# Edges of the adder layers, full-width products beside the projection, and the load order and ending of a scan, in a four-layer kernel on one Trainium2 core

## The chip, the cores and the metric

The kernel runs as one program on one core of one Trainium2 chip. The metric is the device time of one execution in microseconds (us). The profile gives the span from the first to the last instruction, the instructions of each engine, and the granted clock of TensorE. PE is TensorE's matrix products and PEld its weight loads, DVE is VectorE, ACT is ScalarE, POOL is GpSimd, and SP is the engine that issues most DMAs; a letter q behind an engine's name means its DMA queue. On this chip a float32 product is recorded as two passes, so counts of matmuls in the profile are twice those of the source.

## The reference

The input is four images of 128 channels and 64 x 64 pixels, in float32. Four layers follow each other:

```python
# layer 0: attention over the 4096 pixels of an image
attn = softmax(einsum('bci,bcj->bij', q, k)); x = gamma * einsum('bcj,bij->bci', v, attn) + x
# layer 1: twice a 3x3 convolution with weights rounded to powers of two, and an adder convolution
wq  = sign(w) * 2 ** round(log2(abs(w))), zero where abs(w) < 0.005
p   = conv3x3(x, wq)
out = -sum over taps and channels of abs(patch(p) - w_add)          # for each of 128 outputs
out = batchnorm(out)          # statistics over all images and pixels; relu after the first
x   = relu(second out + residual)
# layer 2: layer norms, a depthwise convolution with pooled attention, a feed-forward network
# layer 3: a selective scan
m      = sigmoid(illum_w . [x, illumination] + illum_b);  f_low = x * m
f_high = x * (1 + alpha * gradient)
xs, z  = split(in_proj(rms_norm(f_high)))
xs     = silu(causal_conv1d(xs, 4 taps))
dt, Bm, Cm = x_proj(xs);  delta = softplus(dt_proj(dt) + b)
# a forward and a backward scan of 16 states for each of 256 channels
h = exp(delta * A) * h + delta * Bm * xs;   y = sum over states of h * Cm + D * xs
out = layer_norm(out_proj(y * silu(z))) + gamma * f_low
```

## The kernel before

The layers run one after the other; each holds its data in SBUF and hands over through DRAM tensors (x1d, y1d, y2d, low_d, xs_d, sz_d, delta_d, du_d, xdbl_d, y_d) or, between layers 2 and 3, in four SBUF images `xp`. Channels lie on the 128 partitions, pixels along the free axis, and BK = 512 pixels make one block, 8 blocks one image. Instructions that are wrapped in `then` (keep_in_program_order) keep the order of the source on their engine. Those that are not wrapped, most DMAs of SP among them, are placed by the framework's scheduler before the program is built.

**Layer 1** (`layer1`, `shift_adder`). Both filters are loaded and quantized in `quantized` (L287) and `quantize` (L266 to L278), nine DVE instructions of 128 x 1152 each. `shift_adder` is called twice, with tags a1 and a2. It loads `w_add` (L306), makes negated copies (L311), small selection matrices (L316 to L320) and, on PE, the sums `wsum` of the weights (L335). Then the convolution of the first image runs alone: per block nine products from `xin` into one of three PSUM banks `pc` (L375), copied to the padded image `pb` by DVE (L380). The loop over 4 x 128 outputs follows the hand-written list ORDER. Per output, ACT makes absolute differences (`absolute`, L456), DVE makes maxima (`maximum`, L470; `added`, L462; `pair`, L479), and PE sums each over the channels into the PSUM banks `pa` (`summed`, L425). `pair` makes two half tiles from a ring `am` of seven, and a DMA that POOL issues adds one to the other (L481). Beside this loop a generator `beside` brings in the sums over the image (L396) and the next image's convolution, three steps for every four outputs. `evacuate` adds `wsum`, takes the statistics (L437, L440) and stores the outputs (L442). At the end `batchnorm_scale` sends the statistics to the DRAM tensor stats_d (L543), reads them back in another layout (L546), and aggregates them (L550). The second call normalizes its input blocks as they land (L571 to L575).

**Layer 3's preparation** (`layer3_prepare`). `split(b)` works block by block: one full product with `iwm` (L1053) and a one-row product with the illumination row (L1054) for the sigmoid, a one-row product with the gradient row (L1056), the sigmoid on ACT (L1058), `fh` (L1059) and the low part `sg` (L1061) on DVE, and a store to low_d (L1062). `norm(b)` (L1070 to L1081) is the root-mean-square norm. `project(b)` makes four pieces: products `px` copied to `pre` by ACT (L1099, L1100), four convolution passes of DVE (L1122, L1124), products `pz` through Silu (L1106, L1108) stored to sz_d, and Silu of the piece (L1127). `steps_of(b)` makes `xd` with 40 columns (L1143, L1146), `dv` from its first 8 rows (L1155, L1158), and softplus with Abs, Exp and Ln (L1160, L1161, L1169), and stores delta_d and du_d. For each image `project(b)`, `split(b + 1)` and `steps_of(b)` follow one another; `norm(b + 1)` runs beside the steps. The tiles `dv`, `ee` and `uu` have three buffers each, PSUM eight banks.

**Layer 3's scan** (`layer3_scan`). There are 128 tiles, 32 an image, of 8 channels and 16 states each, with two halves of 2048 pixels. Per half, `delta` loads `dl` and `products_in` loads `du`, spread over the partitions; `inputs` multiplies `du` by B on POOL (L1343). ACT makes the decays `da` (L1350), DVE scans (L1364), PE adds both directions (L1379), ACT copies (L1388), POOL multiplies by C (L1392). Loads are issued on SP in the order of the source. `finish` makes the output blocks (L1455 to L1475) of the image before, and after the last tile those of the last image.

Of the kernel before, what the change touches and what calls it, by code (L numbers as in the profile page):

```python
# [9 lines left out]
F32 = mybir.dt.float32  # L10
# [7 lines left out]
P = 128  # L18
B = 4
# [242 lines left out]
def quantize(nc, sb, w, of, name):  # L262

    flat = [P, TAPS * P]
    aw = sb.tile(flat, F32, tag="qa", name=f"{name}_aw")
    nc.vector.tensor_scalar(aw.bitcast(I32), w.bitcast(I32), 0x7FFFFFFF, None, ALU.bitwise_and)  # L266

    pw = sb.tile(flat, F32, tag="qp", name=f"{name}_pw")
    nc.vector.tensor_scalar(pw.bitcast(I32), w.bitcast(I32), 0x7F800000, None, ALU.bitwise_and)
    up = sb.tile(flat, F32, tag="qu", name=f"{name}_up")  # L270
    nc.vector.scalar_tensor_tensor(up, pw, 1.4142135381698608, aw, ALU.mult, ALU.is_lt)
    nc.vector.scalar_tensor_tensor(pw, up, 1.0, pw, ALU.add, ALU.mult)
    nc.vector.scalar_tensor_tensor(pw, aw, 0.005, pw, ALU.is_ge, ALU.mult)
    sg = sb.tile(flat, I32, tag="qu", name=f"{name}_sg")
    nc.vector.tensor_scalar(sg, w.bitcast(I32), -0x80000000, None, ALU.bitwise_and)
    nc.vector.tensor_tensor(pw.bitcast(I32), pw.bitcast(I32), sg, ALU.bitwise_or)
    nc.vector.tensor_tensor(pw, pw, w, ALU.subtract)
    nc.vector.tensor_tensor(of, w, pw, ALU.add)  # L278


def quantized(tc, pool, w_shift, tag):

    nc = tc.nc
    wqs = pool.tile([P, TAPS, P], F32, name=f"{tag}wq")
    with tc.tile_pool(name=f"{tag}q", bufs=1) as qp:
        ws = qp.tile([P, TAPS * P], F32, name=f"{tag}ws")
        nc.sync.dma_start(ws, w_shift)  # L287
        quantize(nc, qp, ws, wqs.rearrange("p t o -> p (t o)"), tag)
    return wqs


def shift_adder(tc, cm, load, wqs, w_add, stats, y_d, tag):
# [10 lines left out]
    with ExitStack() as ctx:  # L303
        cp = ctx.enter_context(tc.tile_pool(name=f"{tag}c", bufs=1))
        wa = cp.tile([P, TAPS, P], F32, name=f"{tag}wa")
        nc.sync.dma_start(wa.rearrange("p t o -> p (t o)"), w_add)  # L306
        wn = {}
        for t, scale in [(t, 1.0) for t in ABS_TAPS[0]] + [(ABS_TAPS[c][i], 0.5) for c, i in HALF.items()]:
            if (t, scale) not in wn:
                wn[t, scale] = cp.tile([P, P], F32, name=f"{tag}wn{t}_{len(wn)}")  # L310
                nc.vector.tensor_scalar(wn[t, scale], wa[:, t, :], -scale, None, ALU.mult)  # L311

        pick = {}
        for v in (-1.0, -2.0):
            pick[v] = cp.tile([P, 63], F32, name=f"{tag}pick{int(-v)}")
            nc.vector.memset(pick[v], 0.0)  # L316
            nc.vector.memset(pick[v][:, 31:32], v)
        third = cp.tile([P, 32], F32, name=f"{tag}third")
        nc.vector.memset(third, 0.0)
        nc.vector.memset(third[:, 2:32:4], 1.0)  # L320
# [5 lines left out]
        with tc.tile_pool(name=f"{tag}w", bufs=1) as wt:  # L326
            w_third = wt.tile([P, P], F32, name=f"{tag}wthird")
            nc.vector.memset(w_third, 0.0)
            nc.vector.tensor_copy(w_third[:, 2:P:4], wa[:, MAX_TAPS[3], 2:P:4])
            pw = ps_c.tile([P, NC], F32, tag="cv", name=f"{tag}pw")  # L330
            for c in range(NC):
                for g in range(4):
                    for i, t in enumerate(sum_taps):
                        w = w_third if t == MAX_TAPS[3] else wa[:, t, :]
                        nc.tensor.matmul(  # L335
                            pw[32 * g : 32 * g + 32, c : c + 1], w[:, 32 * c : 32 * c + 32], cm.one_col,
                            start=(i == 0), stop=(i == len(sum_taps) - 1), skip_group_check=True,
                        )
            nc.vector.tensor_copy(wsum, pw)
# [64 lines left out]
        def beside(b, pb_of):  # L404

            yield from sums_of_p(b, pb_of[b], sp_of[b])
            if b < B - 1:
                pb_of[b + 1] = padded(b + 1)
                yield from convolution(b + 1, pb_of[b + 1])

        pb_of, sp_of = {0: padded(0)}, {}
        for _ in convolution(0, pb_of[0]):
            pass
# [19 lines left out]
        def evacuate(chunk):  # L433
            b, c = divmod(chunk, NC)
            for k in range(2):
# [6 lines left out]
                nc.sync.dma_start(to[k], o)  # L442

# [29 lines left out]
        def pair(n, h):  # L473
# [7 lines left out]
            then(nc.gpsimd.dma_start(ms[1], ms[0], accum_op=ALU.add))  # L481
# [53 lines left out]
def layer1(ctx, tc, cm, w_shift1, w_add1, g1, b1, w_shift2, w_add2, g2, b2, x1d, y1d, y2d, stats_d):  # L535
# [5 lines left out]
    def batchnorm_scale(stats, at, gamma, name):  # L541

        nc.sync.dma_start(at, stats.rearrange("p c s v -> p c (s v)"))  # L543
        byco = lp.tile([P, 4, 2 * B * 6], F32, name=f"byco{name}")
        for c in range(4):
            nc.sync.dma_start(  # L546
                byco[32 * c : 32 * c + 32], at[:, c, :].rearrange("(g j) s -> j g s", g=4)
            )
# [11 lines left out]
    wq1, wq2 = quantized(tc, lp, w_shift1, "a1"), quantized(tc, lp, w_shift2, "a2")  # L560
# [6 lines left out]
    shift_adder(tc, cm, plain, wq1, w_add1, stats1, y1d, "a1")  # L567
    mean1, sc1 = batchnorm_scale(stats1, stats_d[0], vec["g1"], "1")
# [11 lines left out]
    shift_adder(tc, cm, normed, wq2, w_add2, stats2, y2d, "a2")  # L580
    mean2, sc2 = batchnorm_scale(stats2, stats_d[1], vec["g2"], "2")
# [422 lines left out]
def layer3_prepare(  # L1004
    tc, cm, xp, maps_d, illum_w, illum_wl, illum_b, rms_w, in_w, conv_w, conv_b, x_w, dt_w, dt_b,
    alpha, gamma, low_d, xs_d, sz_d, delta_d, du_d, xdbl_d,
# [3 lines left out]
    with ExitStack() as ctx:  # L1010
# [14 lines left out]
        ga = load([P, 1], gamma.partition_broadcast(P), "ga")  # L1025
# [4 lines left out]
        xw = load([P, 2, NX], x_w, "xw")  # L1030
        dtw = load([DT_RANK, 2 * P], dt_w, "dtw")
# [7 lines left out]

        fh_of, xs_of = {}, {}  # L1040

        def split(b):

            fh = big.tile([P, N], F32, tag="fh", name=f"fh{b}")
            fh_of[b] = fh
# [669 lines left out]
```

## Time and profile before

| | us |
|---|---|
| median of 3 runs | 21133.91 |
| lowest and highest run | 21114.99 and 21178.35 |
| the profiled execution's own time | 21155.93 |
| its span | 21154.1 |

| stage of the profiled execution | from | to |
|---|---|---|
| layer 0 | 0 | 1980 |
| layer 1, start | 1980 | 2025 |
| first adder layer: convolution of image 0, then the loop | 2025, 2091 | 9404 |
| between the adder layers | 9404 | 9438 |
| second adder layer: convolution of image 0, then the loop | 9438, 9504 | 16840 |
| between layer 1 and layer 2 | 16840 | 16889 |
| layer 2 | 16889 | 17883 |
| layer 3, preparation | 17883 | 18520 |
| scan: start, then the loop | 18520, 18574 | 21080 |
| scan: ending | 21080 | 21154 |

Over the whole span PE is busy for 93%, DVE for 90%, ACT for 83% and POOL for 36% of the time, and the mean granted clock is 0.966. These shares are means over stages with different limits; what an edit is worth is read in its own stage. In a line of the order of instructions, the numbers are the start and the length in us, and the bracket at the end gives the engine's idle time just before and what ended it.

### The profile page before, as it was taken

To read this page: it belongs to the slowest core of one execution; us is meant where nothing else is said; L and a number is where in the kernel's file an instruction comes from. 1 tells how busy PE (TensorE), PEld (TensorE's weight loads), DVE (VectorE), ACT (ScalarE), POOL (GpSimd) and SP (SyncE) were. 2 spreads that over 40 slices of the span, in tenths; PEclk is the share of its full clock that TensorE was granted. 3 is DMA by queue.
4 is the path that set the end of the run, shared out by engine and by line. 5 is a ranking of instruction groups with operands and counts; after the bars stand their busy time and mean duration, and the time that the engine had idled before them with its cause. 6 is when DMAs were issued, how large, how long until landed. Compare 5 with 4: busy or idle time off the path is not lost.

```text
span 21154.1 us, 323001 instructions
## 1 busy us (share of the span) xinstructions
PE 19660.1 (93%) x139180; PEld 6292.0 (30%) x139180; DVE 18970.2 (90%) x12273; ACT 17550.0 (83%) x9055; POOL 7577.3 (36%) x3844
## 2 busy tenths in 40 slices
PE   9998999999999999999999999999999877789998
PEld 4443222222222222222222222222222223223333
DVE  7876999999999999989999999999999887799998
ACT  5664999999999999989999999999999833466666
POOL 5665222222222222212222222222222100189998
PEclk9999999999999999999999999999999988699999
DMA  0000777777777777767777777777777710389997
GB/s 13 9 9 20 147 152 148 147 154 149 151 145 152 150 143 151 156 136 145 150 148 152 149 148 151 147 149 147 147 154 153 162 21 20 130 238 251 253 253 218
DMA packets 576191, 2970.17 MB, mean 140 GB/s; under 512 B 164572, under 2 KB 165476, under 8 KB 240804
## 3 DMA queue, kind: packets, MB, share of 16 engines
q0 software_dynamic: 296800, 2160.20, 51.0%
q1 hardware_dynamic: 277812, 787.19, 13.0%
q8 instruction: 1089, 17.84, 0.3%
q14 instruction: 346, 2.83, 0.0%
q10 hardware_dynamic: 144, 2.10, 0.0%
HBM read 662.03 MB, written 128.78 MB: 37 GB/s over the span
## 4 chain that ended last, share of the span: by engine, by line
PE 43%; issue 15%; DMA 14%; DVE 14%; ACT 11%; POOL 3%; SPq 1%; DVEq 0%; POOLq 0%; ACTq 0%
PE a1pa L425 15%; PE a2pa L425 13%; DMA ma<-ma 10%; ACT aa L456 9%; PE pe L164 4%; PE pav L207 4%; DVE h L1364 4%; DVE ma L479 3%; DVE da L470 2%; DMA du<-du_d 2%; DVE g L854 1%; POOL ma L481 1%; PE mg L1379 1%; DMA dl<-delta_d 1%; PE a1pc L375 1%
## 5 line engine op out<-in xcount | busy, mean ns | idle before, releaser
L481 POOL DMA_DIRECT2D ma<-ma x2048 | 3799.7, 1870 | 10892.9 <-DVE ma L479 7671.8
L456 ACT ACTIVATE aa<-a1pb,a1wn 128x4096 f32<-128x4096 f32 x1920 | 6959.4, 3711 | 485.5 <-PE a1pa L425 342.0
L456 ACT ACTIVATE aa<-a2pb,a2wn 128x4096 f32<-128x4096 f32 x1920 | 6964.9, 3712 | 358.9 <-PE a2pa L425 340.4
L425 PE MATMUL a1pa<-aa,a1pick 128*32 128x512 f32 x30720 | 3616.8, 600 | 84.4 <-ACT aa L456 81.3
L425 PE MATMUL a2pa<-aa,a2pick 128*32 128x512 f32 x30720 | 3617.2, 600 | 82.6 <-ACT aa L456 81.3
L470 DVE TENSOR_SCALAR da<-a2pb,a2wa 128x4096 f32<-128x4096 f32 x1408 | 3271.0, 2350 | 316.1 <-PE a2pa L425 316.1
L470 DVE TENSOR_SCALAR da<-a1pb,a1wa 128x4096 f32<-128x4096 f32 x1408 | 3269.6, 2350 | 306.8 <-PE a1pa L425 306.5
L425 PE MATMUL a1pa<-da,a1pick 128*32 128x512 f32 x22528 | 2696.1, 597 | 15.2 <-DVE da L470 15.2
L425 PE MATMUL a2pa<-da,a2pick 128*32 128x512 f32 x22528 | 2680.8, 594 | 18.0 <-DVE da L470 18.0
L479 DVE TENSOR_SCALAR ma<-a1pb,a1wa 128x2048 f32<-128x2048 f32 x2048 | 2529.8, 1282 | 71.1 <-DMA ma<-ma 71.1
L479 DVE TENSOR_SCALAR ma<-a2pb,a2wa 128x2048 f32<-128x2048 f32 x2048 | 2530.6, 1282 | 63.5 <-DMA ma<-ma 63.3
L1379 PE MATMUL mg<-h,ident 128*128 128x512 f32 x4096 | 1955.8, 615 | 214.6 <-ACT m L1388 174.0
L1364 DVE TENSOR_TENSOR_SCAN h<-da,h,dbu 128x1024 f32<-128x1024 f32 x768 | 1804.3, 2349 | 126.1 <-ACT da L1350 32.2
L425 PEld LDWEIGHTS a1pa<-aa,a1pick 128*32 128x32 f32 x30720 | 982.4, 111 | 2492.5 <-issue 2130.5
L425 PEld LDWEIGHTS a2pa<-aa,a2pick 128*32 128x32 f32 x30720 | 983.1, 111 | 2488.0 <-issue 2132.9
L425 PE MATMUL a2pa<-ma,a2pick 128*32 128x512 f32 x8192 | 1094.2, 607 | 266.0 <-DMA ma<-ma 265.8
L425 PE MATMUL a1pa<-ma,a1pick 128*32 128x512 f32 x8192 | 1096.2, 608 | 239.1 <-DMA ma<-ma 239.1
L201 POOL TENSOR_TENSOR ssum<-ssum,et 128x512 f32<-128x512 f32 x960 | 1230.0, 1281 | 233.0 <-ACT et L196 166.1
L425 PEld LDWEIGHTS a1pa<-da,a1pick 128*32 128x32 f32 x22528 | 716.9, 110 | 1747.2 <-issue 1612.4
L425 PEld LDWEIGHTS a2pa<-da,a2pick 128*32 128x32 f32 x22528 | 714.8, 110 | 1739.7 <-issue 1584.1
L462 DVE SCALAR_TENSOR_TENSOR aa<-a2pb,a2wa,aa 128x4096 f32<-128x4096 f32 x256 | 1147.4, 4482 | 81.8 <-ACT aa L456 81.7
L462 DVE SCALAR_TENSOR_TENSOR aa<-a1pb,a1wa,aa 128x4096 f32<-128x4096 f32 x256 | 1147.4, 4482 | 78.2 <-ACT aa L456 78.0
(295 smaller groups left out, 17707.1 us busy)
## 6 DMA issues: line engine op xcount, KB each, us to landing
ma<-ma POOLq DMA_DIRECT2D x2048, 1024.0 KB, 8.9
dl<-delta_d SPq DMA_DIRECT2D x256, 512.0 KB
dl<-delta_d SPq DMA_DIRECT2D x512, 256.0 KB
du<-du_d SPq DMA_DIRECT2D x256, 512.0 KB
du<-du_d SPq DMA_DIRECT2D x512, 256.0 KB
sz_d<-sz SPq DMA_DIRECT2D x64, 256.0 KB
xs_d<-xs SPq DMA_DIRECT2D x8, 2048.0 KB
delta_d<-dv SPq DMA_DIRECT2D x32, 512.0 KB
```

The lines of the kernel that those rows point to most:

```text
L164: nc.tensor.matmul(pe, k[:, bass.ts(j, P)], unit[u, "q"], start=True, stop=True)
L201: nc.gpsimd.tensor_tensor(unit[u, "sum"], unit[u, "sum"], at, ALU.add)
L207: nc.tensor.matmul(unit[u, "av"], image[u // NB][2][:, j, :], at, start=(j == 0), stop=(j == NJ - 1))
L375: then(nc.tensor.matmul(pc, wqs[:, t, :], here[:, y : y + RB, x : x + W], start=(t == 0), stop=(t == TAPS - 1),))
L425: then(nc.tensor.matmul(pa[k][32 * g : 32 * g + 32, :], pick[v][:, 31 - jj : 63 - jj], d[:, bass.ts(4 * at + g, BK)], start=(n // 32, k) n ...
L456: then(nc.scalar.activation(rows(at), view(n, t), AF.Abs, bias=bias, scale=scale))
L462: then(nc.vector.scalar_tensor_tensor(rows(at), view(n, ADDED_TAP), weight(n, ADDED_TAP), rows(at), ALU.max, ALU.add))
L470: then(nc.vector.tensor_scalar(rows(dt), view(n, t), weight(n, t), None, ALU.max))
L479: then(nc.vector.tensor_scalar(rows(mt), v, weight(n, t), None, ALU.max))
L481: then(nc.gpsimd.dma_start(ms[1], ms[0], accum_op=ALU.add))
L1364: then(nc.vector.tensor_tensor_scan(t[:, cols][:, s], da[:, s], st[n, "dbu", h][:, cols][:, s], 0.0 if e % 4 == 0 else st["last"], ALU.mul ...
L1379: then(nc.tensor.matmul(pm, cm.ident, st[n, way, h][:, bass.ts(k, BK)], start=(way == 0), stop=(way == 1)))
```

## The change

In layer 1, `quantize` becomes a generator that works in the ring `am`. Only the first layer's filter is quantized before the first convolution; the second layer's goes in four lots into that convolution, and `w_add`, its negated copies and `w_third` are loaded and made there. The sums of the weights become a generator `sums_of_w` in `beside` of image 0. The last output's pair is not added by a DMA: both half tiles are summed by PE. The statistics go by DMA from `stats` straight into `byco` in SBUF, chunk by chunk, and the last chunk's on two queues. `stats_d` is gone.

In layer 3's preparation, one-row products and those with 8 rows or 40 columns are made full-width with zeros: `xw`, `dtw`, `iwr`, `alr` and four map rows are zero-filled tiles of 128 rows. `split` is divided: `high(b)` makes only `fh`, into the image `xp[b - 1]` that is no longer needed, and for the next image stands in `project`, two blocks a piece; `low(b)` makes all eight sigmoid products, then the sigmoids in ACT and the product on POOL, and for the next image stands at the end of `project`. The factor gamma moves to the end of the scan.

In the scan, the first loads come in another order, and the last image's output has an ending of its own.

```diff
-def quantize(nc, sb, w, of, name):
+def quantize(tc, pool, w_shift, of, name):
+    w, aw, pw, up = [
+        pool.tile([P, HL], F32, tag="am", name=f"{name}_q{k}")[:, 0 : TAPS * P] for k in range(4)
+    ]
+    nc.sync.dma_start(w, w_shift)
+    yield
+    then(nc.vector.tensor_scalar(aw.bitcast(I32), w.bitcast(I32), 0x7FFFFFFF, None, ALU.bitwise_and))
...
         def beside(b, pb_of):
 
             yield from sums_of_p(b, pb_of[b], sp_of[b])
+            if b == 0:
+                yield from sums_of_w(w_third)
...
-        for _ in convolution(0, pb_of[0]):
-            pass
+        quantizing = [quantize(tc, mp, w, of, f"{tag}{k}") for k, (w, of) in enumerate(shifts)]
+        for q in quantizing[:1]:
+            for _ in q:
+                pass
+        for at, _ in enumerate(convolution(0, pb_of[0])):
+            if at == 0:
+                nc.sync.dma_start(wa.rearrange("p t o -> p (t o)"), w_add)
+                for q in quantizing[1:]:
+                    next(q)
+            if at % TAPS == 4 and at > 2 * TAPS:
+                for q in quantizing[1:]:
+                    next(q, None)
+            if at == 2 * TAPS + 1:
+                negated()
...
+            if b == B - 1:
+
+                for g in range(4):
+                    (nc.scalar if c == NC - 1 and g % 2 else nc.sync).dma_start(
+                        byco[32 * c : 32 * c + 32, g, :],
+                        stats[32 * g : 32 * g + 32, c, :, :].rearrange("p s v -> p (s v)"),
+                    )
...
-            then(nc.gpsimd.dma_start(ms[1], ms[0], accum_op=ALU.add))
+            if n < B * P - 1:
+                then(nc.gpsimd.dma_start(ms[1], ms[0], accum_op=ALU.add))
+            else:
+
+                streams[n, "q", h] = (-2.0, ms[0], (h,))
             streams[n, "p", h] = (-2.0, ms[1], (h,))
...
-        nc.sync.dma_start(at, stats.rearrange("p c s v -> p c (s v)"))
-        byco = lp.tile([P, 4, 2 * B * 6], F32, name=f"byco{name}")
-        for c in range(4):
-            nc.sync.dma_start(
-                byco[32 * c : 32 * c + 32], at[:, c, :].rearrange("(g j) s -> j g s", g=4)
-            )
...
+        def padded(shape, name):
+            t = cp.tile(shape, F32, name=name)
+            nc.gpsimd.memset(t, 0.0)
+            return t
+
+        xw = padded([P, 2, P], "xw")
+        nc.sync.dma_start(xw[:, :, 0:NX], x_w)
+        dtw = padded([P, 2 * P], "dtw")
+        nc.sync.dma_start(dtw[0:DT_RANK, :], dt_w)
...
+        map_rows = [[padded([P, BK], f"map{i}_{j}") for j in range(2)] for i in range(2)]
+
+        def map_row(i, b, k):
+            t = map_rows[i][k % 2]
+            nc.sync.dma_start(t[0:1, :], maps_d[i, b, bass.ts(k, BK)].rearrange("(o n) -> o n", o=1))
+            return t
...
+        def low(b):
+
+            halves = []
+            for k in range(NB):
+                pm = ps.tile([P, BK], F32, tag="mm", name=f"pm3_{b}_{k}")
+                then(nc.tensor.matmul(pm, iwm, inner(xp, b, k), start=True, stop=False))
+                then(nc.tensor.matmul(pm, iwr, map_row(0, b, k), start=False, stop=True))
+                halves.append(pm)
+            yield
+            for k2, tag in enumerate(("dv", "ee", "uu", "dv")):
+                sg = sb.tile([P, 2 * BK], F32, tag=tag, bufs=3, name=f"sg{b}_{k2}")
+                for i in range(2):
+                    then(nc.scalar.activation(sg[:, bass.ts(i, BK)], halves[2 * k2 + i], AF.Sigmoid, bias=ib))
+                src = xp[b][:, 2 * RB * k2 : 2 * RB * (k2 + 1), :].rearrange("p h w -> p (h w)")
+                then(nc.gpsimd.tensor_tensor(sg, src, sg, ALU.mult))
+                nc.sync.dma_start(low_d[b, :, bass.ts(k2, 2 * BK)], sg)
+
+        def high(b):
+
+            if b == 0:
+                fh = big.tile([P, N], F32, tag="fh", name="fh0")
+            else:
+                fh = xp[b - 1].rearrange("p h w -> p (h w)")
             fh_of[b] = fh
             for k in range(NB):
...
+                pg = ps.tile([P, BK], F32, tag="mm", name=f"pg{b}_{k}")
+                then(nc.tensor.matmul(pg, alr, map_row(1, b, k), start=True, stop=True))
                 yield
-                then(nc.vector.scalar_tensor_tensor(rows(sg), src, ga, rows(sg), ALU.mult, ALU.mult))
-                nc.sync.dma_start(low_d[b, :, c], sg)
+                then(nc.vector.scalar_tensor_tensor(
+                    rows(fh[:, bass.ts(k, BK)]), rows(pg), 1.0, inner(xp, b, k), ALU.add, ALU.mult
+                ))
...
-        def project(b):
+        def project(b, beside, behind):
...
                 if i + 1 < len(pieces):
                     projected(*pieces[i + 1])
+                next(beside, None)
+                next(beside, None)
...
                 for k in range(NB // 2):
                     gated(mc, h * NB // 2 + k)
+                if i + 1 == len(pieces):
+                    next(beside, None)
+                    next(behind, None)
                 then(nc.scalar.activation(xc, xc, AF.Silu, bias=cb[:, mc : mc + 1]))
                 if h == 1:
                     nc.sync.dma_start(xs_d[b, mc], xs_of[b, mc])
+            next(behind, None)
...
-        for _ in split(0):
+        for _ in high(0):
             pass
         cm.ln_and_exp(tc)
         for _ in norm(0):
             pass
+        for _ in low(0):
+            pass
         for b in range(B):
-            project(b)
-            if b < B - 1:
-                for _ in split(b + 1):
-                    pass
+            more = b < B - 1
+            project(b, high(b + 1) if more else iter(()), low(b + 1) if more else iter(()))
...
         for h in range(2):
-            delta(0, h)
             products_in(0, h)
             by_states(0, 0, h)
-        for h in range(2):
+            delta(0, h)
             inputs(0, h)
+        products_in(1, 0)
+        delta(1, 0)
+        products_in(1, 1)
+        for h in range(1, -1, -1):
             by_states(0, 1, h)
-            products_in(1, h)
...
-        going, k, t = [], 0, 0
-        while going or k < NB:
...
+        for k in range(NB + 1):
+            v = f"_last{k}"
+            if k < NB:
+                ck = bass.ts(k, BK)
+
+                t = big.tile([P, 4, BK], F32, tag="h", bufs=6, name=f"end{v}")
+                moved(t[:, 2, :], low_d[B - 1, :, ck])
+                for c in range(2):
+                    moved(t[:, c, :], y_d[B - 1, c, :, ck])
...
+                sq = sb.tile([P, BK], F32, tag="rs4", bufs=4, name=f"sq{v}")
+                then(nc.scalar.activation(sq, po, AF.Square))
+                then(nc.vector.tensor_scalar(t[:, 2, :], t[:, 2, :], ga, lb, ALU.mult, ALU.add))
+                ends[k] = (t, po, sq)
+            if k > 0:
...
+                then(nc.scalar.activation(rs, pv, AF.Ln, bias=cm.eps))
+                then(nc.scalar.activation(rs, rs, AF.Exp, scale=-0.5))
+                then(nc.vector.scalar_tensor_tensor(t[:, 3, :], po, lw, rs, ALU.mult, ALU.mult))
+                then(nc.vector.tensor_tensor(t[:, 3, :], t[:, 3, :], t[:, 2, :], ALU.add))
+                nc.gpsimd.dma_start(out[B - 1, :, bass.ts(k - 1, BK)], t[:, 3, :])
```

## The prediction

> **What bounds the kernel now.** I read first the busy time by stage, then the order of instructions on each engine at every seam between stages, then the list of waits in layer 3's preparation. By stage (start:end and length in us; then busy us of PE, PEld, DVE, ACT, POOL; granted clock, DMA share, GB/s):
>
> ```profile
> 1980.00:2025.00 45.00, 7.82 (x192) 7.69 (x193) 22.26 (x34) 0.00 (x0) 0.80 (x6) 0.50 0.20 60
> 2091.00:9404.00 7313.00, 6981.32 (x62224) 2043.94 (x62228) 6855.90 (x3804) 6960.51 (x1921) 1874.26 (x1059) 0.98 0.74 150
> 9404.00:9438.00 34.00, 12.81 (x228) 8.45 (x220) 7.65 (x23) 2.25 (x4) 1.68 (x7) 0.59 0.47 104
> 9504.00:16840.00 7336.00, 6970.93 (x62232) 2040.05 (x62236) 6873.55 (x3829) 6979.87 (x1944) 1932.36 (x1059) 0.99 0.74 149
> 16840.00:16889.00 49.00, 4.40 (x32) 0.57 (x24) 13.78 (x18) 6.54 (x5) 1.35 (x3) 0.55 0.71 244
> 17990.00:18018.00 28.00, 28.00 (x31) 7.89 (x30) 8.68 (x13) 7.37 (x10) 0.00 (x0) 0.50 0.38 151
> 18520.00:18574.00 54.00, 9.98 (x16) 4.36 (x16) 21.68 (x30) 9.76 (x9) 18.00 (x4) 0.52 0.98 246
> 18574.00:21080.00 2506.00, 2313.47 (x6760) 799.02 (x6760) 2378.18 (x1078) 1731.16 (x2159) 2339.95 (x555) 0.99 0.89 246
> 21080.00:21154.00 74.00, 36.21 (x81) 11.04 (x80) 1.38 (x2) 25.51 (x41) 24.74 (x17) 0.76 0.36 121
> ```
> The two adder loops (7313 and 7336 us) and the scan (2506 us) hold 17155 of 21154 us; in the loops PE, ACT and DVE are each at 94 to 95%. The change leaves these loops' instructions alone but for a few products. It works on the seams, where the engines wait: 45, 34, 49, 54 and 74 us, and on layer 3's preparation (17883 to 18520). There the order on PE reads:
>
> ```profile
> 17897.76 2.08 PE L1053 MATMUL pm<-x,iwm 128*128 128x512 f32 x2
> 17899.77 2.07 PE L1054 MATMUL pm<-mr,iwr 1*128 1x512 f32 x2
> 17901.63 1.91 PE L1056 MATMUL pg<-mr,alr 1*128 1x512 f32 x2
> ...
> 17933.12 3.78 PE L1074 MATMUL pv<-sq,mean 128*128 128x512 f32 x4 [1.01 <-ACT sq L1070]
> ```
> A block of `split` takes 5.71 us of PE, without a gap; its six passes take 0.95 us each. In the projection 16 such passes take 7.03 us, 0.43 each. So `split` is PE-bound at half clock: PE is busy for 28.00 of 28 us and the clock is 0.50. Two thirds of its products have one row. At layer 1's seams the waits are on transfers:
>
> ```profile
> 9426.16 1.02 DVE L550 BATCH_NORM_AGGREGATE mv<-byco 128x2 f32<-128x192 f32 x1 [0.58 <-DMA byco<-stats_d]
> 9432.85 71.13 SPq L571 DMA_DIRECT2D a2xin<-y1d  x11
> 9438.45 65.03 PE L375 MATMUL a2pc<-a2xin,a2wq 128*128 128x512 f32 x144 [5.67 <-ACT a2xin L575]
> 16878.51 2.41 DVE L673 TENSOR_SCALAR x<-x,mv,sc 128x4096 f32<-128x4096 f32 x1 [6.44 <-DMA x<-y2d]
> ```
>
> **Layer 1's start: -30.** Now: x1d's last block at 1980.1, the first filter lands and is quantized by 1994.87, then the second (14.2 us), then w_add (3.7) and its sums (8.2 of PE), then the input block (4.0); the convolution starts at 2025.02. After: only the first quantizing stands ahead, the input lands beside it, and the convolution starts at 1994.9. The second filter's nine DVE passes (10.4 us) go into the convolution, where DVE works 5.79 of 66 us, in four lots of about 3 us. A `pc` copy queued behind a lot is at most 3 us late, three banks of 7.7 us each cover that, and PE goes on; without the cover it would be 4 x 3 us. w_add is asked for after three input blocks and is wanted 17 us later. Bounds -33 to -27.
>
> **The sums of w inside the loops: +10.** 96 products (192 passes, 8.2 us) for each of two layers now stand among the adder products, on a PE that is 95% busy. Nothing if they fall into its gaps, 17 if each pushes the end. The chain of waits goes over PE more than over any other engine, so I take above half. They run in the first 20 of 92 side steps, and 93 fit, so the next image's convolution is still in time.
>
> **First to second adder layer: -18.** The last pair is no longer added by a transfer (9406.08 to 9413.27) but by 8 passes more for each half (1.04 us each), so the last statistics are ready at about 9410.8, not 9416.77. Then they went to DRAM (issued 9416.84), came back (9423.03), and were aggregated at 9426.16; now four issues on two queues (0.44 us each) go to SBUF straight and land, like `iw` (2.1 us from issue), at 9413.5. With 1.02 + 0.29 + 1.28 + 0.35 us the scale is there at 9416.5. The input block can be asked for when y1d's last store has landed, 9413.7 (issued at 9411, 2.7 us as `delta_d`'s takes), lands in 3.9 and is normalized in 1.5: PE starts at 9419, not 9438.45. I take 18 of the 19; the bounds are 10 (the store takes the 6.2 us that stats_d took, and more) and 22. [...]
>
> **Second adder layer to layer 2: -14.** The flush is 6 us shorter in the same way. SP's load of image 0 (16869.77) stood behind the DRAM round trip (16863.85); now 13 loads of 0.5 us stand ahead of it, so it goes out near 16853.5, and lands 8.7 us later as now, or up to 4 more beside `res`. Bounds -18 to -5.
>
> **Layer 3's preparation: -77.** *Image 0, -6.* `high(0)` is 8 products of 1.9 us, each waiting for one row in one of two buffers (2.3 us from issue): 4.2 us for two, 17 for all, instead of 46. Eight POOL fills (about 4 us, by 0.23 for 132 columns) fit in the time of the loads. `norm(0)` stays. `low(0)` then adds 32 passes, 14 us at 0.43, that `split` had inside; and the first convolution waits for the first `pg`, queued behind 8 projections: 4.5 us. 29 - 14 - 4.5, with 4 lost to cold passes: -6. *Three transitions, -65.* Image 3 has no `split` behind it: from the last convolution pass (18445.74) to the first `Abs` (18449.28) it takes 3.5 us; image 1 takes 40.3 (18138.77 to 18179.07). So a `split` costs 36.8. After: 8 `fh` passes inside `project` (8 x 0.69 = 5.5, DVE being the bound there: 52.2 of 53 us), and ACT's table load and 8 sigmoids at its end (1.28 + 8 x 0.69 = 6.8); `low`'s 32 passes lie under ACT's and DVE's last piece. The product moves to POOL (4 x 2.34 us), idle there. That is -24.5; I take off 3 for new waits: `fh` waits for its map row, with the four passes of the piece behind it and ACT's Silu waiting for those; a row waiting on SP for its buffer holds back sz_d stores, for which ACT waits (46.3 us today); the third `dv` waits for `sg`'s store. *Full-width steps, -6:* `pxd` and `pd` at 0.95 a pass lose some 1 to 2 us for each of 3 parts and 4 images, where DVE waits for them. Bounds -30 (rows late in each piece) to -105 (6 + 3 x 24.5 + 25).
>
> [...]
>
> **The scan's start: -2.** The first product needs `du` and B; `dl` goes behind them, so the first scan starts some 6 us sooner. But the DMA share is 0.98 from 18520 to 18574, and the twelve loads before tile 1's second half are the same bytes. What is won is waited for there. Bounds -8 to +4.
>
> **The scan's end: -22.** Now two blocks at a time wait for loads (PE 2.7 to 5.7 us each time), and end at 21148.7 plus 5.4 for the last store. After, loads run six blocks ahead: 8 x 768 KB at 240 GB/s is 26 us from 21090, against PE's 3.0, ACT's 1.9 and DVE's 2.0 a block. Then 7 us for the last block, and 7 for a store from POOL (the least for `ma` is 6.9): 21131, not 21154. Bounds -28 to -10.
>
> Sum: -30 + 10 - 18 - 14 - 77 - 2 - 22 = -153; with every bound at its worst -61, at its best -214. The profiled execution took 21155.93 (span 21154.1), 22 above the median 21133.91 of the runs; I take the sum off the median: 20981.
>
> **The rivals.** *The clock stays at half in spite of the zeros* (for: the added rows do no work; against: `pxd`, 128 rows by 40, brings 0.45 a pass at 18025). `low(0)` then costs 15 more, each hidden `low` 10, the steps win nothing: -153 + 51 = -102, 21032. *Rows, stores and banks hold the preparation* (for: 46.3 us of Silu waiting for sz_d; against: SP issued rows between stores in `split`). Each later piece waits 8 us for its rows, 72 in all, and `low`'s rows come behind the last store, 13 us three times: -153 + 111 = -42, 21092. *The adder loop gets slower* by its order: the quantizer takes eight tiles of the `am` ring of seven, so layer 1's pairs sit one buffer on, and the sums delay PE, and three engines at 95% do not catch up. Its price is per channel: 1024 channels of 14.3 us; from 0.15 us each (1.0%) it eats the whole gain, from 0.21 the kernel is slower by over 0.3%. For it: the two layers' loops differ by 23 us with the same code; against it: that is 0.04 us a channel. At 0.25 it is 21237.
>
> **How the numbers follow.** A run of this kernel can tell 0.3%, 63 us, from no change. The forecast has 0.67, the clock 0.14, the held preparation 0.11, the slower loop 0.06; 0.02 stays for more than all of it. The forecast alone spans 20920 to 21073; reaching to the held preparation, and with 15 us of the runs' spread below, 20905 to 21090. Faster: the first two and the rest, 0.83; within 0.3%: most of the held preparation, 0.10; slower: the loop and a worse hold, 0.07.
>
> **What would show it.** Right: convolutions at 1995 and near 9394 (9419 less 30, and 5 for the sums), loops still 7313 to 7345 us, one-row products gone and the clock above 0.8 in the projection, no stretch between image 1's last convolution pass and its first `Abs` above 17 us, a tail of 50 us. Wrong: a loop longer by 60 us, `fh` waiting for `pg` by over 5 us a piece, or POOL fills or the last store on the chain.

## The result and the profile after

The changed kernel is slower, by little: 21181.64 us as the median of 20 runs (21154.04 to 21223.47), against 21143.69 for 20 runs of the kernel before, ratio 1.0019 with a 95% interval of 1.0012 to 1.0025. The forecast was 20981 us. The profiled execution took 21184.28 us (span 21182.5), 28.4 more than the profiled one of before in span.

The same view as before, busy time by stage (start:end and length in us; busy us of PE, PEld, DVE, ACT, POOL; granted clock, DMA share, GB/s), of the changed kernel:

```profile
1980.00:1996.00 16.00, 0.27 (x1) 0.30 (x2) 10.24 (x9) 0.00 (x0) 0.99 (x12) 0.50 0.69 186
2064.00:9461.00 7397.00, 6986.45 (x62452) 2050.77 (x62456) 6851.48 (x3803) 6955.81 (x1919) 1929.60 (x1058) 0.98 0.74 148
9461.00:9477.00 16.00, 2.02 (x21) 0.54 (x14) 5.20 (x8) 4.13 (x6) 1.06 (x12) 0.69 0.42 112
9545.00:16964.00 7419.00, 7000.82 (x62452) 2051.29 (x62456) 6869.87 (x3828) 6975.80 (x1944) 1979.10 (x1058) 0.98 0.73 148
...
18032.00:18048.00 16.00, 14.61 (x34) 6.07 (x34) 1.52 (x4) 8.33 (x12) 7.03 (x3) 1.00 0.20 82
...
21116.00:21182.50 66.50, 43.20 (x109) 14.83 (x107) 16.68 (x26) 18.72 (x30) 14.36 (x11) 0.76 0.40 135
```

The seams did shrink. But each adder loop now takes about 7400 us, 84 more than before, and DVE and ACT have no more work in it. Of the 168 us of both loops together, 138 are more idle time of PE and 30 more busy time: what grew is mostly waiting. By marks that both traces have (first adder product, the start of the last chunk's first evacuation, the first normalization of layer 2, its last `pf` product, the first and the last scan), the 28.4 us are made up so:

| stretch | before, us | after, us | measured | forecast |
|---|---|---|---|---|
| up to the first adder product | 2094.6 | 2063.9 | -30.6 | -30 |
| first loop | 7313.3 | 7397.3 | +83.9 | +10 for both |
| first to second adder layer, with the convolution | 100.1 | 84.1 | -16.0 | -18 |
| second loop | 7334.6 | 7418.8 | +84.2 | (above) |
| second adder layer to layer 2 | 35.9 | 28.8 | -7.1 | -14 |
| layer 2 | 1004.6 | 1008.3 | +3.7 | 0 |
| preparation, up to the first scan | 660.5 | 590.9 | -69.6 | -77 and -2 |
| scans | 2526.2 | 2523.4 | -2.8 | 0 |
| behind the last scan | 84.3 | 67.0 | -17.3 | -22 |

Without the loops the sum is -140, where -163 was forecast. The loops took back 168, and they did it in one place. Cut at the evacuations, image 0 of the two layers goes from 1884.8 and 1897.8 us to 1978.6 and 1989.3 (+94 and +92), and images 1 to 3 together from 5428.5 and 5436.9 to 5418.7 and 5429.5. The windows of one chunk in image 0 and one in image 1 show it; of before:

```profile
2612.00:3064.00 452.00, 441.10 (x3892) 131.00 (x3888) 428.47 (x239) 434.91 (x121) 110.98 (x66) 0.99 0.76 153
...
4448.00:4906.00 458.00, 441.64 (x3896) 131.13 (x3892) 429.24 (x240) 435.68 (x121) 121.93 (x66) 0.99 0.75 152
```
and of after:

```profile
2620.00:3100.60 480.60, 443.62 (x3892) 130.46 (x3888) 428.86 (x241) 435.12 (x121) 135.83 (x67) 0.97 0.72 144
...
4512.00:4962.50 450.50, 438.58 (x3892) 131.09 (x3888) 428.70 (x239) 435.16 (x121) 111.60 (x66) 1.00 0.77 154
```
The chunk of image 0 has 28.6 us more, though PE works only 2.5 us more and DVE and ACT no more; POOL, which makes nothing new there, has 25 us more. Only image 0 has `sums_of_w`.

In ORDER a token names an output of a group of four, a kind and an index: 1P1 is output 1's pair (P) for half 1 of the image, M a maximum, S the maximum added to an absolute difference, A an absolute difference, and C the place of the three side steps; a small letter is PE's sum of the same. "Held" is said here of an issue of the adding DMA that takes POOL over 8 us. How a stall of PE comes about is read from the order of instructions (start, length, what; in the bracket the idle time before and what ended it). DVE of after:

```profile
2682.89 0.69 DVE L377 COPY a1pb<-a1pc 128x512 f32<-128x512 f32 x1 [2.63 <-PE a1pc L372]
...
2699.59 4.61 DVE L491 TENSOR_SCALAR da<-a1pb,a1wa 128x4096 f32<-128x4096 f32 x2
2704.11 2.48 DVE L500 TENSOR_SCALAR ma<-a1pb,a1wa 128x2048 f32<-128x2048 f32 x2
2706.50 4.62 DVE L491 TENSOR_SCALAR da<-a1pb,a1wa 128x4096 f32<-128x4096 f32 x2
...
2720.34 2.35 DVE L491 TENSOR_SCALAR da<-a1pb,a1wa 128x4096 f32<-128x4096 f32 x1
```
POOL's issues of the adding DMA, and PE, at the same time:

```profile
2695.58 0.86 POOL L503 DMA_DIRECT2D ma<-ma  x1 [4.83 <-DVE ma L500]
2707.12 17.47 POOL L503 DMA_DIRECT2D ma<-ma  x3 [10.69 <-DVE ma L500]
```
```profile
2729.09 1.93 PE L439 MATMUL a1pa<-ma,a1pick 128*32 128x512 f32 x8 [10.27 <-DMA ma<-ma]
```
DVE copies a block of image 1's convolution right behind its last product and waits 2.63 us for it. From there on it runs without a pause. POOL's issue for pair 1P1 (the first of the three in the 17.47 us) begins at 2707.12 and ends at 2722.8, when DVE's run ends: 15.7 us, and PE stands for 10.27. The clock falls with it: it is granted at 0.5 from 2722.38 to 2732.61, so the eight passes at 2729.09 take 1.93 us where eight like them took 1.04 at 2707.48. At the same place of ORDER in the kernel before, an earlier group, DVE and then POOL:

```profile
2186.95 2.35 DVE L470 TENSOR_SCALAR da<-a1pb,a1wa 128x4096 f32<-128x4096 f32 x1
2189.52 2.35 DVE L470 TENSOR_SCALAR da<-a1pb,a1wa 128x4096 f32<-128x4096 f32 x1 [0.23 <-PE a1pa L425]
```
```profile
2180.41 11.58 POOL L481 DMA_DIRECT2D ma<-ma  x2 [10.45 <-DVE ma L479]
```
There DVE waits 0.23 us for PE, and the issue ends in that gap, after 9.0 us; PE stands for 2.7. In image 0 the changed kernel has 11 and 9 stalls of PE of 9 to 12 us, the kernel before none. Added up over both loops, PE stood for 287 us before products of 1P1 whose issue had been held, and for 102 in the kernel before; in image 0 of the two layers it is 209 against 19, and image 0 is 185 us longer.

Why the copy stands there: `beside` is advanced by three steps at each token C. Before, 12 steps of `sums_of_p` came ahead of image 1's convolution, so every copy fell on the first step of a token, a whole group of four outputs behind its product. The eight steps of `sums_of_w` make that 20, and every copy of image 1 falls on the third step, behind products given out in the same token.

### The profile page after: what moved, and what is told of

Its sections match the earlier page's. It is cut to its first block, busy times and chain, and to the rows that moved or that the text cites. A ratio compares the mean times of both kernels' runs of the same rounds, so it can differ in the third digit from the quotient of the medians.

```text
span 21182.5 us, 323113 instructions
## 1 busy us (share of the span) xinstructions
PE 19563.3 (92%) x139212; PEld 6293.6 (30%) x139212; DVE 18961.4 (90%) x12251; ACT 17547.3 (83%) x9043; POOL 7699.6 (36%) x3870
## 5 line engine op out<-in xcount | busy, mean ns | idle before, releaser
L503 POOL DMA_DIRECT2D ma<-ma x2044 | 3898.9, 1923 | 10909.8 <-DVE ma L500 7737.4
```

## The experiments

Three theories stood against each other: A, the place of the copies, by way of the held issues; B, the sums' products themselves or the new addresses; C, the prediction's rival, the `am` ring moved on by the quantizer's tiles. Medians of the kernel before differ by chip, 21045 to 21144 us, so ratios to runs of it on the same chip are compared.

**Nine steps in place of eight.**
```diff
                     if g % 2:
                         yield
+            yield
             then(nc.vector.tensor_copy(wsum, pw))
```


> The changed kernel with one empty side step more in sums_of_w (nine in place of eight), so that image 1's evacuations fall on the first of the three side steps of a C token again, as in the kernel before. All products stay in the loop. Theory A (place of the copy): the eight steps put each evacuation a1pb, a2pb right behind its own last product, DVE waits 2.6 us there, loses its pauses, GpSimd's accumulate issue is held for 15.7 instead of 9 us, and PE stalls 10.3 instead of 3 us. Then both loops, first product to last chunk's evacuation, go from 7397 and 7419 us back towards 7313 and 7335, at least the 61 and 68 us lost after the first chunk; total 21015 to 21065. Theory B (the 96 products, their one-column form or the pools' new addresses cost the time): no change, 21180. Theory C (the prediction's rival, the am ring moved by the quantizer's eight tiles): no change in layer 1's first loop, 21180.

Measured: ratio 0.9958 (0.9946 to 0.997), 20974.68 us against 21071.46. Image 0 took 1894.7 and 1914.5 us. Its chunk that had 480.6 us reads

```profile
2589.00:3039.00 450.00, 440.73 (x3896) 130.21 (x3892) 428.41 (x239) 435.00 (x121) 112.22 (x66) 0.99 0.76 154
```
Behind the first chunk, image 0 had lost 55 and 68 us, and nine steps won back 52 and 47 of them. An empty step turned the change from slower into faster. Theories B and C are out: the products, the addresses and the ring are as in the changed kernel.

**Only the place, in the kernel before.**
```diff
             yield from sums_of_p(b, pb_of[b], sp_of[b])
+            if b == 0:
+                yield
+                yield
```


> The kernel before with two empty side steps in image 0 between sums_of_p and the convolution: nothing is added but the place of image 1's evacuations, now on the third side step of a C token as in the changed kernel. Theory A: each loop longer by 50 to 85 us, almost all of it in the first four chunks, total 21245 to 21310; stalls of PE of 10.3 us about every 177 us. Theories B and C: no change, 21144.

Measured: ratio 1.0055 (1.0043 to 1.0067), 21196.96 us against 21071.46. The profile has 7 stalls of 9 to 12 us in image 0 of each layer, which takes 1922.2 and 1951.9 us, 53 and 58 more than in the kernel with layer 1 as before (below) on the same chip; the loops are 38 and 49 us longer than there, less than the 50 to 85 expected. By the medians two empty steps slow a kernel that is otherwise unchanged by 125 us, three quarters of the 168 that the changed kernel's loops lost.

**Only the copy, one step later.**
```diff
                 for t in range(TAPS):
+                    if t == later and made:
+                        evacuated()
...
-                then(nc.vector.tensor_copy(pb[:, 1 + RB * k : 1 + RB * (k + 1), 1 : 1 + W], rows(pc)))
+                made.append((k, pc))
+                if later == 0 or k == NB - 1:
+                    evacuated()
...
-                yield from convolution(b + 1, pb_of[b + 1])
+                yield from convolution(b + 1, pb_of[b + 1], later=int(b == 0))
```


> The changed kernel, eight steps as they are, so that every product of TensorE keeps its place; only the DVE copy of an evacuation of image 1 is given out one side step later, before the second product of the next piece, which is the first side step of the next C token. Theory A: as with nine steps, 21015 to 21065, and DVE's waits for a1pc in image 0 go from about 2.6 us each to none. If it is the place of the products in TensorE's queue that counts and not the copy's: 21180. Theories B and C: 21180.

Measured: ratio 0.9953 (0.9941 to 0.9965). What DVE and PE waited for from 2600 to 3900 us (total us, times, longest), in the changed kernel:

```profile
DVE a1pb L377 <- PE a1pc L372: 15.8, 6, 2.6
```
```profile
PE a1pa L439 <- DMA ma<-ma: 72.6, 11, 10.4
```
and with the copy later:

```profile
DVE a1pb L367 <- PE a1pc L380: 2.6, 1, 2.6
```
```profile
PE a1pa L449 <- DMA ma<-ma: 32.8, 15, 3.9
```
TensorE's products stand where they stood; moving the copies alone is enough.

**Layer 1 as before, the rest as changed.**
```diff
-def quantize(tc, pool, w_shift, of, name):
+def quantize(nc, sb, w, of, name):
...
-            if b == 0:
-                yield from sums_of_w(w_third)
...
-    shift_adder(tc, cm, plain, wq[0], shifts, w_add1, stats1, byco[0], y1d, "a1")
+    shift_adder(tc, cm, plain, wq1, w_add1, stats1, y1d, "a1")
```


> The changed kernel with layer 1 as in the kernel before (quantize, shift_adder, layer1); layer 3's preparation and the scan as changed. From the two traces: layer 3's preparation 660.5 to 590.9 us, the scan with its end 2610.5 to 2590.3, layer 2 1004.6 to 1008.3: total 21144 - 70 - 20 + 4 = 21058 if all the loss lies in layer 1's loops. If the preparation or the scan loses in other runs what it gains in the profiled one: above 21100.

Measured: ratio 0.9963 (0.9951 to 0.9975), 73 us under 21071.46: the gain of layer 3 is real, and all that was lost lies in layer 1. Image 0 took 1869.1 and 1894.0 us, so with nine steps the sums themselves cost up to 26 and 21 us there, as profiles of single executions tell it.

**Layer 3 without the zeros** (on nine steps, as the next).
```diff
-        xw = padded([P, 2, P], "xw")
-        nc.sync.dma_start(xw[:, :, 0:NX], x_w)
+        xw = load([P, 2, NX], x_w, "xw")
...
-        map_rows = [[padded([P, BK], f"map{i}_{j}") for j in range(2)] for i in range(2)]
+        map_rows = [[cp.tile([1, BK], F32, name=f"map{i}_{j}") for j in range(2)] for i in range(2)]
```


> The kernel with nine steps, in layer 3's preparation without the zeros: the rows of the maps, alr and iwr have one partition again, xw 40 columns, dtw 8 rows; the order is as changed and the eight POOL fills are gone. If width sets the clock there (the prediction): products at 0.95 us a pass where they are at 0.43 now, low(0) longer by about 15 us, each of the three transitions by up to 10, the steps by 6, the fills' 4 us saved; total 20 to 50 us over the nine steps. [...]

Measured: ratio 0.9971 (0.996 to 0.9983) beside 0.9958, too near to tell alone; the stage tells. Preparation takes 621.7 us, not 592.8: +14.8 up to the first convolution pass, +5.9, +3.4 and +3.3 in the transitions, nothing in the steps. PE with zeros (changed kernel), then without:

```profile
18032.75 1.02 PE L1082 MATMUL pm<-x,iwm 128*128 128x512 f32 x2
18033.61 1.02 PE L1083 MATMUL pm<-map,iwr 128*128 128x512 f32 x2
```
```profile
17818.36 1.02 PE L1081 MATMUL pm<-x,iwm 128*128 128x512 f32 x2
17819.31 1.12 PE L1082 MATMUL pm<-map,iwr 1*128 1x512 f32 x2
...
17826.68 2.04 PE L1081 MATMUL pm<-x,iwm 128*128 128x512 f32 x2
17828.65 2.07 PE L1082 MATMUL pm<-map,iwr 1*128 1x512 f32 x2
```
Two full-width passes of this stretch take 0.86 to 0.97 us from one start to the next, but for a wait of 1.39 us for a map row. With a one-row product in every pair they begin at 0.95 to 1.06 and take 1.97 some 8 us later, on a PE without a gap. The granted clock of that stretch, without the zeros:

```profile
17818.00:17826.60 8.60, 8.60 (x18) 2.37 (x16) 1.51 (x3) 5.22 (x7) 2.34 (x1) 1.00 0.00 1
17826.60:17840.00 13.40, 13.40 (x15) 3.46 (x14) 0.00 (x0) 2.75 (x4) 4.68 (x2) 0.51 0.29 118
```
PE is busy for all of both, and the clock still falls from 1.00 to 0.51; with the zeros it is 1.00 over the 16 us from 18032 to 18048 of the changed kernel. In this stretch one-row products bring the half clock and the zeros avoid it, as the prediction had it. Behind a wait of 5.09 us, at 18237.73, two passes of the changed kernel take 2.08 us in spite of the zeros.

**The scan's start and ending as before.**
```diff
-            products_in(0, h)
-            by_states(0, 0, h)
             delta(0, h)
-            inputs(0, h)
+            products_in(0, h)
+            by_states(0, 0, h)
...
-        ends = {}
-        for k in range(NB + 1):
+        going, k, t = [], 0, 0
+        while going or k < NB:
```


> The kernel with nine steps, the scan's first loads and its ending as in the kernel before (gamma stays at the end, in finish). The prediction's terms: -2 for the start and -22 for the end, so 24 us over the nine steps; the two traces of before and after have the scan with its end at 2610.5 and 2590.3, so 20 us over. If loads bound the ending in either form: no difference.

Measured: ratio 0.997 (0.9958 to 0.9982). By stage: preparation up to the first scan 596.3, not 592.8 (the start: 3.5 us), and 84.6, not 66.3, behind the last scan (the ending: 18.3 us).

**Pair 1P1 ahead of 1S1, in the changed kernel and with nine steps.**
```diff
-    ... 1P0 -1p1 1A2 1S1 0m0 1a0 0p0 1A3 1M1 1a2 1a1 1M0 0p1 2A0 1m1 1P1 1a3 ...
+    ... 1P0 -1p1 1A2 1P1 1S1 0m0 1a0 0p0 1A3 1M1 1a2 1a1 1M0 0p1 2A0 1m1 1a3 ...
```


> The changed kernel, with its eight steps, and in ORDER the token 1P1 moved from behind 1m1 to just before 1S1. In the changed kernel 33 of 256 accumulate issues of pair 1P1 are held over 8 us (26 of them over 12), each behind a run of DVE TENSOR_SCALARs without a pause; no issue that fell into a SCALAR_TENSOR_TENSOR was held over 1.3 us. Moved, the issue falls into 1S1. Theory A (the copy's wait costs time through the held issue of this pair): the stalls of 10.3 us are gone although DVE still waits 18.4 us for the copies in image 0; both loops come back to 7270 to 7345 us, total 21000 to 21060 against 21181 on the first chip. If the copy's waits cost the time by themselves, or through DVE's order: no gain; if moving the pair only moves the held issue to 2P1 (14 us to the next SCALAR_TENSOR_TENSOR): stalls of 4 to 8 us there and no gain or a loss.

> Nine steps and the moved token 1P1 together, the candidate for a version faster than both. With nine steps 10 issues of 1P1 are still held over 8 us and the PE waits for ma over 1.5 us sum to 394 us over both loops. Theory A: those of 1P1 go, some 50 to 80 us; total 20890 to 20930 where nine steps alone has 20975. If the held issue moves on to 2P1: 20975 or slower.

Measured: ratios 1.0776 (1.0762 to 1.0791) and 1.0833 (1.0818 to 1.0848). No issue of 1P1 is held any more (mean 0.86 us) and no wait of PE for `ma` is longer than 6.7 us, but the first kernel's loops grew to 8112 and 8189 us. In layer a1's loop of the first of the two, from 2620 to 9990 us, DVE and PE now waited for

```profile
DVE ma L500 <- DMA ma<-ma: 668.8, 179, 7.9
```
```profile
PE a1pa L439 <- DVE aa L483: 647.3, 116, 10.2
```
The pair needs its tiles before the ring of seven has them back, and `aa`, behind it, is late. The edit brought a larger wait of its own and settles nothing on the held issues.

**A short instruction as an opening.** A SCALAR_TENSOR_TENSOR on a 128 x 8 scratch tile, behind one, two or three places:
```diff
             make[kind](n, i)
+            if (n % 4, kind, i) in ((2, "M", 1),):
+                then(nc.vector.scalar_tensor_tensor(opened, opened, 1.0, opened, ALU.mult, ALU.max))
```


> The changed kernel, eight steps and its copies behind their products, with one SCALAR_TENSOR_TENSOR of 128 x 8 (a scratch tile onto itself) given to DVE behind the maximum 2M1, the first instruction after pair 1P1. It costs DVE 256 short instructions and moves nothing else. Theory A: GpSimd's issue for 1P1 gets through at that instruction, so none of the 256 is held over 8 us (33 in the changed kernel), PE's stalls of 10.3 us are gone though DVE still waits 18.4 us for copies in image 0 of each layer, image 0 goes from 1979 and 1989 us to 1900 to 1930, and the total is 15 to 70 us under the kernel before. If the wait for the copies costs the time by itself: image 0 stays at 1979 and 1989. If a short instruction doesn't let GpSimd through, or one boundary is not enough: no change, or up to 30 us more.

> Nine steps and the same short instruction behind 2M1. Nine steps alone has ratio 0.9958 to the kernel before, with 10 issues of 1P1 held over 8 us. Theory A: these go, at 7 us each less the cost of the short instructions: 0.992 to 0.996. Otherwise 0.996 to 0.998.

> Nine steps and the short instruction at two places, behind 2M1 and behind pair 0P1, since 68 of 256 issues of pair 0P0 are held for 9 us until the next SCALAR_TENSOR_TENSOR and PE then waits about 3 us. Theory A: both kinds of held issue go, PE's waits for ma over 1.5 us fall from 394 us to under 150, ratio 0.982 to 0.992. If PE does not use the time (ACT and DVE at 95% are as late): the same as with one place.

> Nine steps and the short instruction at three places: behind 2M1, behind pair 0P1, and behind 2M0, which follows pair 2P1. With two places 11 issues of 2P1 were still held for over 12 us. Theory A: these go too, some 7 us of stall each less 256 x 0.16 us of DVE time, so ratio 0.970 to 0.976 to the kernel before; with two places it is 0.9756. If the short instructions' own time on DVE outweighs what is left, or the held issue moves on to 2P0: 0.976 to 0.980.

| | ratio to before | 1P1, 2P1, 0P0 held over 8 us | PE waits for `ma` over 1.5 us, both loops |
|---|---|---|---|
| before | 1 | 18, 0, 69 | 446 us |
| changed | 1.0019 | 33, 0, 57 | 561 us |
| nine steps | 0.9958 | 10, 0, 68 | 394 us |
| changed, behind 2M1 | 0.9951 (0.9939 to 0.9964) | 0, 24, 48 | 410 us |
| nine steps, behind 2M1 | 0.9933 (0.9919 to 0.9947) | 0, 12, 63 | 371 us |
| and behind 0P1 | 0.9756 (0.9743 to 0.977) | 0, 11, 0 | 125 us |
| and behind 2M0 | 0.9729 (0.9716 to 0.9743) | 0, 0, 0 | 41 us |

(The counts and sums are taken over all instructions of each trace; of the 446 us of before, 12 lie behind the loops, where the last pair is waited for.) The changed kernel with the one place shows the middle link: it keeps the eight steps, DVE still waits 18.4 us for copies in image 0 of each layer, yet the stalls of 9 to 12 us are gone and image 0 takes 1918.4 and 1922.7 us. From 2600 to 3900 us its trace has

```profile
DVE a1pb L379 <- PE a1pc L374: 18.4, 7, 2.6
```
```profile
PE a1pa L441 <- DMA ma<-ma: 49.3, 9, 7.3
```
The total is 104 us under the kernel before, more than the 15 to 70 expected. So most of what was lost went by the issue that the copy's wait keeps shut out. A rest stays: with this place open, eight steps are still 44 us behind nine (20967.93 against 20923.5 on one chip), and PE waits 39 us longer for `ma`. How much of the 44 is the copies' wait by itself was not separated. The instruction is cheap (ns, least, median, most):

```profile
L521 DVE SCALAR_TENSOR_TENSOR a1opened<-a1opened x128: 150/158/166, 2096.2 to 9321.5; 128x8 f32<-128x8 f32 x128
```
Closing one place moved some held issues to the next, 2P1, at a lower price: PE stood 7.3 us before each product of the 24, and 8.7 before each of the 33 of 1P1. With three places the first loop takes 7043.9 us, and the wait that led it in the changed kernel,

```profile
PE a1pa L439 <- DMA ma<-ma: 307.7, 78, 10.4
```
is down to (both over layer a1's loop)

```profile
PE a1pa L442 <- DMA ma<-ma: 44.5, 34, 2.6
```
The gain of the second place, 1.8%, was larger than expected: ACT and DVE were not the bound that their 95% suggested. Of the 371 us by which it shortens the two loops, 254 are idle time of PE and 117 busy time, at a granted clock of 0.994 and 0.997 in place of 0.989 and 0.986. The kernel with three places takes 20472.88 us against 21052.2 of the kernel before on its chip, the fastest version seen.

## Why the prediction was wrong, and where it was right

**The step that failed** is "The sums of w inside the loops: +10", and in it the sentence "They run in the first 20 of 92 side steps, and 93 fit". It priced the 96 products on PE and asked whether the steps fit, not where the steps behind them then fall. In its place the runs showed a wait: the steps behind the sums moved, DVE's copies came right behind their own products, issues of 1P1 were held, and PE stood for their transfers. With nine steps, and the same products, the two loops together are 12 us longer than those of the kernel with layer 1 as before on the same chip, so the price of the products was about right; with eight they cost 168 us, 0.164 us a channel. A loop longer by 60 us was the prediction's own sign of being wrong. Of the +94 and +92 us in image 0, nine steps won back 84 and 75, but 31 and 28 of this lie in the first chunk, where no copy of image 1 stands.

**The third rival** named the right side and nearly the price ("from 0.15 us each it eats the whole gain"), with the wrong mechanism: the ring is moved in layer a1 alone, and a2 lost as much; and nine steps leave the ring moved. Its chance of 0.06 was too small for a change that reorders what three engines at 95% do.

**Layer 1's start, -30,** and **the first seam, -18,** came near the forecast, -30.6 and -16.0. One part of the seam was mis-sized: the statistics were to be in `byco` 2.7 us behind the last BATCH_NORM_STATS2, and DVE waited 7.70:

```profile
9472.12 1.02 DVE L568 BATCH_NORM_AGGREGATE mv<-byco 128x2 f32<-128x192 f32 x1 [7.70 <-DMA byco<-stats]
```

**The second seam, -14,** gave 7.1. The step that was off is that four issues on two queues go out at once. ACT's queue (`res` is a load of 2 MB), and SP's load of image 0:

```profile
16965.88 0.38 ACTq L690 DMA_DIRECT2D res<-x1d  x1
16980.29 1.17 ACTq L460 DMA_DIRECT2D byco<-stats  x2
```
```profile
16984.94 2.25 SPq L691 DMA_DIRECT2D x<-y2d  x4
```
ACT's two issues of `byco` go out 14.4 us behind `res`. By the semaphores of the trace they were released when SP's second copy of `byco`, issued at 16968.68, had landed, at 16980.21, beside the 2 MB. So the statistics are aggregated at 16983.79, 17 us behind the last BATCH_NORM_STATS2. On SP, too, one load waited 5.2 us for `res`; image 0, asked for at 16984.94, goes out 20.8 us behind the chunk's evacuation, not 11.

**Layer 3's preparation, -77 and -2,** gave 69.6. The clock was the right reading: its rival, at half clock in spite of the zeros, is out, and the zeros alone bring 28.9 us. Sizes were off in three terms: up to the first convolution pass -12.4 (68.1 to 55.7), not -6; the three transitions -53, not -65 (from the first convolution pass to the first `Abs` 75.1, 76.3 and 77.0 us became 56.7, 59.2 and 59.4; the gap behind the last pass is 19 to 20 us, where 12 to 17 were expected); and the full-width steps nothing, not -6 (76.4, 77.1, 76.6 became 76.4, 77.1, 77.7). No run shows the 4 us that image 0's term has for cold passes, an estimate of the author's: `low(0)`'s 32 passes began at 18032.75 and the next product at 18048.36, at a clock of 1.00 and with one wait of 1.39 us, and `high(0)`'s first eight took 6.31 us, where eight at full clock take 3.60 (18107.26).

**The scan's start and end, -2 and -22,** gave 3.5 and 18.3 when each was undone.

Without the failed step the forecast would have had the right sign and too large a size: with one empty step the change has ratio 0.9958, and the prediction's 20981 is 0.9928 of 21133.91.

## What to carry to other kernels

When a generator feeds side work into a loop by a fixed number of steps, count inserted steps modulo that number: here copies right behind their own products made DVE wait 2.6 us each, and the price was paid by PE, 10.3 us at a time. In this kernel an issue of GpSimd's adding DMA could take as long as DVE ran TENSOR_SCALARs back to back (15.7 us at 2707.12); in the kernel before one ended in a gap of 0.23 us, after 9.0 us, and none that began in a SCALAR_TENSOR_TENSOR took over 1.28 us. A short SCALAR_TENSOR_TENSOR behind the critical issues was worth far more than its time (0.16 us each; three places, 2.3% of the kernel over the nine steps alone). Equal busy times with a longer stage (28.6 us in one chunk here) mean a wait: look for it by image and chunk before costing instructions again.

## What the runs showed of the hardware

How long GpSimd took to issue the adding DMA depended on what DVE ran. Over both loops of the changed kernel, 357 of the adding DMA's issues began while DVE ran a SCALAR_TENSOR_TENSOR, and none took over 1.28 us; 386 began while it was idle, none over 2.95; of 1300 that began in a TENSOR_SCALAR, 92 took over 8 us and the longest 15.93. A TENSOR_SCALAR of 128 x 4096 takes 2.35 us, a SCALAR_TENSOR_TENSOR of that shape 4.48; why the one holds an issue and the other does not, no trace shows. An issue can be held past the end of the instruction it began in: the one at 2707.12 was not let in at eight boundaries between TENSOR_SCALARs that followed without a gap, and ended after 15.7 us. What decides whether an issue gets in at the next boundary (the one at 2688.66 did, in 2.09 us) is open.

The same order runs differently from one execution to the next. The changed kernel, the one with nine steps and the one with the later copy give out the same instructions up to the end of the sums, yet the first chunk of layer a1 took 556.0, 524.5 and 544.7 us in their profiles. Of the loss in image 0, 39 and 23 us lie in the first chunk, which varies by as much. They can't be the place of the copies, for the first copy of image 1 comes at 2682.89, behind that chunk's end at 2620. They are waits for `ma` all the same: 50.0 and 36.7 us of PE in the first chunk, 15.3 and 17.7 in the kernel before, with 4 and 3 held issues of 1P1 that cost 41 and 24 us there and 3 and 3 that cost 8 and 8. Why the same order holds an issue longer in one execution than in another is open.
